# Four graph layers on one core: transposed edges and repeated 1/sums moved from TensorE to DMA, and a fixed row of turns

## The chip, the cores and the metric

The kernel runs on one core of one Trainium2 chip. The metric is the time of one execution on the device in microseconds. Before the change it was 2764.22 us, the median of three runs (2763.69 to 2765.53).

## What is computed

There are 64 graphs with 256 nodes each and 256 features per node, with a symmetric 0/1 matrix of edges `adj` for every graph. Four layers follow each other, and behind each stands x = layernorm(x + layer(x)). All data are f32.

```
# layer 0: attention with 4 heads of 64; masked by adj; output projection; layer norm with gamma, beta
attn = softmax(where(adj == 0, NEG, q @ k.T * 64**-0.5));  out = (attn @ v) @ Wo.T + bo
# layer 1: layer norm; attention with 8 heads of 32, q = k = v = normed x; then an MLP
x = x + attention(layer_norm(x));  x = x + gelu(layer_norm(x) @ W1 + b1) @ W2 + b2        # 256 -> 1024 -> 256
# layer 2: one head; scores leaky_relu(s1[n] + s2[m]), masked, softmax, times Wh = x @ W
# layer 3: one head; scores leaky_relu((x * a0) @ x.T), masked, softmax, times x
```

The reference's layer 3 has four kinds of edges, of which this input has one.

## The kernel before

The kernel takes the graphs in 32 groups of G = 2. `P` is 128, `N` and `D` are 256, `QB` = 2 blocks of 128 nodes per graph, `TB` = 4 blocks per group, `T` = 512 nodes per group and `NC` = 2 chunks of 128 features. Scores are kept with the keys on the partitions, so that the product with v needs no transposition: a softmax is exp, times the mask, and division by the sum afterwards. A group is a Python generator that writes out instructions up to its next `yield`; several groups are run in turns, so that their instructions stand interleaved in the engines' queues. TensorE's order is tied to the order of the program.

The mask is the matrix of edges with the keys first. `adjb` is `adj` in bf16. TensorE transposes it, and VectorE takes the smaller of it and its transpose; the sum tells whether it is symmetric:

```python
pt = ps_m.tile([P, G, QB, N], BF16, name="pm")          # PSUM
for t in range(TB):
    i, q = divmod(t, QB)
    for kc in range(QB):
        transpose(pt[:, i, kc, q * P:(q + 1) * P], adjb[:, t, kc * P:(kc + 1) * P], identb)
mask = act.tile([P, G, QB * N], BF16, name="mask")
nc.vector.scalar_tensor_tensor(mask, pt, 1.0, adjb, ALU.mult, ALU.min, accum_out=both_ways[:, g:g + 1])
yield from rest("mask")
```

In layer 0 each chunk of features holds m = 2 heads. The products with v go into `po[:, 0]`, and the sums of the exponentials into `po[:, 1]`, by a weight `pick` that has a one in column c:

```python
for n, c in enumerate(cs):                              # both chunks of one graph
    po = ps_m.tile([P, 2, N], F32, name="pm")
    ...  # 8 matmuls of 32 rows each: po[r:r + 32, 0, :] from v and e
    for kc in range(QB):
        for h in range(m):
            z = (2 * h + kc) * 32
            matmul(po[z:z + 32, 1, :], pick[:, c, :], es[n][:, h, kc * N:(kc + 1) * N], start=True, stop=True)
    nc.scalar.copy(oT[:, c, :], po[:, 0, :])
    if c == 0:
        nc.scalar.copy(sums, po[:, 1, :])               # zs
    else:
        nc.vector.tensor_tensor(sums, sums, po[:, 1, :], ALU.add)
```

Then the sums are brought to the nodes' partitions, added up, inverted, repeated 64 times for each head, and transposed back, so that `oT` (features first) can be multiplied by them. It is followed by the projection with `woT`:

```python
def behind(i, oT, zs):                                  # layer 0, one graph
    pz = sums_of(zs)                                    # 2 transposes of 128x128
    r = r_0[:, g * G + i]
    nc.vector.tensor_reduce(r..., pz..., AX.X, ALU.add)
    nc.vector.reciprocal(r, r)                          # 128x8
    rr = att.tile([P, QB, D], F32, name="rr")
    nc.vector.tensor_copy(rr..., r...to_broadcast([P, QB * 4, 64]))
    yield
    pr = ps_m.tile([P, NC, N], F32, name="pm")
    for c in range(NC):
        for q in range(QB):
            transpose(pr[:, c, q * P:(q + 1) * P], rr[:, q, c * P:(c + 1) * P], ident)
    nc.vector.tensor_tensor(oT, oT, pr, ALU.mult)
    yield
    ...  # matmuls of oT with woT, then statistics, scaling, two layer norms (z, xb)
```

The matmul with W2 adds b2 by a matmul with `onesb` and a row `b2m` at the end of every block's sum. The groups are started every 15 turns, and each running group gets one step per turn; `rest` puts empty steps in:

```python
PACE = 15
REST = {"xn": 1, "e3": 2, "products 4": 1, "wh": 2, "mask": 2, "products 2": 1, "xT2": 1}
...
while waiting or running:
    if waiting and step % PACE == 0:
        running.append(waiting.pop(0))
        if waiting:
            next(waiting[0])                            # the loads of the next group
    for r in list(running):
        if next(r, END) == END:
            running.remove(r)
    step += 1
```

Behind the MLP a group goes through layers 2 and 3 as one piece: transposition, a projection (`wx`), scores and mask in `qT`, product with the values, statistics and scaling to `xn`, each for both graphs. At the very end a small test of all sums and edges decides whether a general version of the program has to run as well; with this input it does not.

Of the kernel before, what the change touches and what calls it, by code (L numbers as in the profile page):

```python
# [16 lines left out]
P = 128  # L17
N = 256
# [16 lines left out]
PACE = 15  # L35

REST = {"xn": 1, "e3": 2, "products 4": 1, "wh": 2, "mask": 2, "products 2": 1, "xT2": 1}
# [358 lines left out]
def usual_input(ctx: ExitStack, tc: tile.TileContext, a: dict, out: bass.AP, flag: bass.AP):  # L396
# [5 lines left out]

    nc = tc.nc
# [8 lines left out]
    ps_m = ctx.enter_context(tc.tile_pool(name="ps_m", bufs=4, space=bass.MemoryType.PSUM))  # L412

# [3 lines left out]
    identb = const.tile([P, P], BF16, name="identb")  # L417
    nc.vector.tensor_copy(identb, ident)
    mhalf = const.tile([P, 2 * TB], F32, name="mhalf")
    nc.gpsimd.memset(mhalf, -0.5)  # L420

    pick = const.tile([P, NC, 32], F32, name="pick")
    nc.gpsimd.memset(pick, 0.0)
    for c in range(NC):
        nc.gpsimd.memset(pick[:, c, c:c + 1], 1.0)
# [12 lines left out]
    r_0 = const.tile([P, B, QB, 4], F32, name="r_0")  # L438
# [116 lines left out]
    def to_psum(src, c):  # L555

        pt = ps_m.tile([P, T], F32, name="pm")
        for t in range(TB):
            transpose(pt[:, t * P:(t + 1) * P], src[:, t, c * P:(c + 1) * P], ident)
        return pt  # L560

    def transposed(src, scale=None, bias=None):

        dst = act.tile([P, NC, T], F32, name="xT")
        for c in range(NC):
            pt = to_psum(src, c)
            if scale is None:
                nc.scalar.copy(dst[:, c, :], pt)
            else:
                nc.scalar.activation(dst[:, c, :], pt, AF.Identity, bias=bias[:, c:c + 1], scale=scale[:, c:c + 1])  # L570
        return dst
# [30 lines left out]
    def products(i, cs, v, es, hd, oT, sums, gamma=None):  # L602

        m = P // hd
        for n, c in enumerate(cs):
            po = ps_m.tile([P, 2, N], F32, name="pm")
            for kc in range(QB):  # L610
                for r in range(0, P, 32):
                    h = r // hd
                    e = es[n * (m // 2) + h // 2]
                    matmul(po[r:r + 32, 0, :], v[:, i * QB + kc, c * P + r:c * P + r + 32],
                           e[:, h % 2, kc * N:(kc + 1) * N], start=kc == 0, stop=kc == QB - 1)
            if gamma is not None:
                nc.scalar.activation(oT[:, c, :], po[:, 0, :], AF.Identity, scale=gamma[:, c:c + 1])
                continue
            for kc in range(QB):
                for h in range(m):  # L620
                    z = (2 * h + kc) * 32
                    matmul(po[z:z + 32, 1, :], pick[:, c, :], es[n][:, h, kc * N:(kc + 1) * N], start=True, stop=True)
            nc.scalar.copy(oT[:, c, :], po[:, 0, :])
            if c == 0:
                nc.scalar.copy(sums, po[:, 1, :])
            else:
                nc.vector.tensor_tensor(sums, sums, po[:, 1, :], ALU.add)

    def sums_of(zs):

        pt = ps_m.tile([P, QB, P], F32, name="pm")
        for q in range(QB):
            transpose(pt[:, q, :], zs[:, q * P:(q + 1) * P], ident)
        return pt

    def rest(where):

        for _ in range(REST.get(where, 0)):
            yield

    def attention(qT, kT, v, mask, hd, gamma, behind):
# [13 lines left out]
        for i in range(G):  # L655
            for cs in ((0, 1),) if m == 2 else ((0,), (1,)):
# [11 lines left out]
                before = (i, cs, v, es, hd, oT, zs, gamma)  # L668
                yield
                for _ in rest(f"scores {m}"):  # L670
                    go_on()
                    yield
# [3 lines left out]
        yield from rest(f"products {m}")  # L676
# [4 lines left out]
    def project(dst, srcT, w, extra, row=None):  # L681
# [3 lines left out]
        for i in range(G):  # L685
            pm = ps_m.tile([P, QB, D], F32, name="pm")
            for q in range(QB):
                t = i * QB + q
                for c in range(chunks):
                    matmul(pm[:, q, :], srcT[:, c, t * P:(t + 1) * P], w[:, c, :],  # L690
                           start=c == 0, stop=c == chunks - 1 and row is None)
                if row is not None:
                    matmul(pm[:, q, :], onesb, row, start=False, stop=True)
                if chunks > NC:
                    yield
            o = dst[:, i * QB:(i + 1) * QB, :]
            if extra is None:
                nc.scalar.copy(o, pm)
            else:
                nc.vector.tensor_tensor(o, pm, extra[:, i * QB:(i + 1) * QB, 0:D], ALU.add)  # L700

    def layer0(g, x, mask):
# [19 lines left out]

        def behind(i, oT, zs):
            pz = sums_of(zs)
            r = r_0[:, g * G + i]
            nc.vector.tensor_reduce(r.rearrange("p q (c h) -> p q c h", c=NC),
                                    pz.rearrange("p q (h k z) -> p q z h k", h=2, k=QB)[:, :, 0:NC], AX.X, ALU.add)
            nc.vector.reciprocal(r, r)

            rr = att.tile([P, QB, D], F32, name="rr")  # L730
            nc.vector.tensor_copy(rr.rearrange("p q (h d) -> p (q h) d", d=64),
                                  r.rearrange("p q h -> p (q h)").unsqueeze(2).to_broadcast([P, QB * 4, 64]))
            yield
            pr = ps_m.tile([P, NC, N], F32, name="pm")
            for c in range(NC):
                for q in range(QB):
                    transpose(pr[:, c, q * P:(q + 1) * P], rr[:, q, c * P:(c + 1) * P], ident)
            nc.vector.tensor_tensor(oT, oT, pr, ALU.mult)
# [20 lines left out]
        yield from attention(qT, kT, v, mask, 64, None, behind)  # L759
        return xb, z  # L760

    def layer1(xb, z, mask):
# [34 lines left out]
        yield from project(x2, hT, w2, both, b2m)  # L797
        return (yield from renormed(x2))

    def renormed(y, var=None):  # L800
# [3 lines left out]
        for i in range(G):  # L804
# [5 lines left out]
        yield from rest("xn")  # L810
        return xn

    def values_of(e, v, one, x, rs, var=None):

        y = act.tile([P, TB, D], F32, name="y")
        for t in range(TB):
# [9 lines left out]
        return (yield from renormed(y, var))  # L826

    def layer2(x, mask):
        xT = transposed(x)
        yield  # L830
        yield from rest("xT2")
# [3 lines left out]
        for tb in range(TB):  # L835
# [5 lines left out]
        yield from rest("wh")  # L841
# [3 lines left out]
        nc.scalar.activation(ex, wh[:, :, D:D + 3], AF.Exp)  # L845
        pt = ps_m.tile([P, G, N], F32, name="pm")
        for t in range(TB):
            transpose(pt[:, t // QB, t % QB * P:(t % QB + 1) * P], ex[:, t, 0:1].to_broadcast([P, P]), ident)
        e = act.tile([P, G, QB, N], F32, name="qT")
        for t in range(TB):  # L850
            i, kc = divmod(t, QB)
            nc.vector.tensor_scalar(e[:, i, kc, :], pt[:, i, :], ex[:, t, 1:2], ex[:, t, 2:3], ALU.mult, ALU.max)
        nc.vector.tensor_tensor(e.rearrange("p g k q -> p (g k q)"), e.rearrange("p g k q -> p (g k q)"),  # L853
                                mask.rearrange("p g k -> p (g k)"), ALU.mult)
        yield
        return (yield from values_of(e, wh, D + 3, x, small.tile([P, TB], F32, name="r")))

    def layer3(g, x, mask):
        xT = act.tile([P, NC, T], F32, name="xT")
        xa = act.tile([P, NC, T], F32, name="z")  # L860
        for c in range(NC):
            pt = to_psum(x, c)
            nc.scalar.copy(xT[:, c, :], pt)
            nc.scalar.activation(xa[:, c, :], pt, AF.Identity, scale=a0[:, c:c + 1])
        yield
        ps = ps_s.tile([P, G, QB, N], F32, name="ps")
        for i in range(G):
            for kc in range(QB):
                for c in range(NC):
# [5 lines left out]
        nc.scalar.activation(e, ps, AF.Exp, bias=shift)  # L875
        nc.scalar.activation(low, ps, AF.Exp, bias=shift, scale=SLOPE)  # L876
        nc.vector.tensor_tensor(e, e, low, ALU.max)  # L877
        nc.vector.tensor_tensor(e.rearrange("p g k q -> p (g k q)"), e.rearrange("p g k q -> p (g k q)"),
                                mask.rearrange("p g k -> p (g k)"), ALU.mult)
        yield  # L880
        yield from rest("e3")
        return (yield from values_of(e, x, D, x, r_3[:, g], last[:, g]))

    def group(g):
# [8 lines left out]
        pt = ps_m.tile([P, G, QB, N], BF16, name="pm")  # L893
        for t in range(TB):
            i, q = divmod(t, QB)
            for kc in range(QB):
                transpose(pt[:, i, kc, q * P:(q + 1) * P], adjb[:, t, kc * P:(kc + 1) * P], identb)
# [4 lines left out]
        yield from rest("mask")  # L902
        xb, z = yield from layer0(g, x, mask)
        x = yield from layer1(xb, z, mask)
        x = yield from layer2(x, mask)
        x = yield from layer3(g, x, mask)
        nc.sync.dma_start(out[g * G:(g + 1) * G].rearrange("b (q p) d -> p (b q) d", p=P), x[:, :, 0:D])
# [59 lines left out]
    waiting = [group(g) for g in range(B // G)]  # L967
    next(waiting[0])
    preparing = prepare()
    running = []  # L970
    step = 0
    while waiting or running:
        if waiting and step % PACE == 0:
            running.append(waiting.pop(0))
            if waiting:
                next(waiting[0])
        for r in list(running):
            if next(r, END) == END:
                running.remove(r)
        step += 1  # L980
        if step >= PREPARE:
            next(preparing, END)
# [4 lines left out]
    nc.vector.tensor_reduce(tops[:, 0:1], r_0.rearrange("p b q h -> p (b q h)"), AX.X, ALU.add)  # L987
# [49 lines left out]
```

## Time and profile before

| engine | busy us | share of the span |
|---|---|---|
| TensorE matmul (PE) | 2678.1 | 97% |
| TensorE weight load (PEld) | 1842.3 | 67% |
| VectorE (DVE) | 1932.5 | 70% |
| ScalarE (ACT) | 1294.7 | 47% |
| GpSimd (POOL) | 576.8 | 21% |

The profile is of one execution with a span of 2764.3 us. A row of the timeline or of the groups names the line of the kernel, the engine and the operation, then the output and the input with their shapes. All matmuls come from one helper (L521) and all transposes from another (L524), so they are told apart by the names of the tiles: `pm<-ident,rr` is a transposition of `rr`. A matmul of f32 stands as two records. The DMA engines moved 57.78 MB, 21 GB/s over the span, and nearly all of that load in the steady state is x, adj and out.

### The profile page before, as it was taken

Reading aid. Unit: us, or ns where it says so; the run is one execution under the profiler, and the core shown is the slowest. Engines: PE = TensorE matmul, PEld = TensorE weight load, DVE = VectorE, ACT = ScalarE, POOL = GpSimd, SP = SyncE. Lnnn points to the kernel's source line nnn. Section 1 sums busy time; section 2 is a strip of 40 time slices with the busy share of each in tenths; the row PEclk is TensorE's granted clock in tenths of the full one; section 3 lists DMA queues with packets and bytes.
Section 4 is the critical chain, followed back from the end, with each engine's and each line's share of the span. In section 5 each row is a group of like instructions: output and inputs, shape, how many; then the busy total and the mean of one; then the engine's idle time right before and its main releaser. Section 6 shows DMA issues by size and latency. Waiting matters only on the chain.

```text
span 2764.3 us, 45617 instructions
## 1 busy us (share of the span) xinstructions
PE 2678.1 (97%) x17288; PEld 1842.3 (67%) x17288; DVE 1932.5 (70%) x6346; ACT 1294.7 (47%) x1953; POOL 576.8 (21%) x1138
## 2 busy tenths in 40 slices
PE   6999999999999999999999999999999999999986
PEld 3666666666666767666667666666666666666664
DVE  5667776777676777766777767677767776767754
ACT  3444544544544444544445445445444445444441
POOL 1112121221221221212221222222212212222211
PEclk8999999999999999999999999999999999999998
DMA  4000000000000000000000000000000000000000
GB/s 126 16 8 24 16 24 16 24 16 16 24 21 19 16 24 16 24 16 24 16 24 16 24 16 24 16 20 20 24 16 17 23 16 24 9 16 9 9 8 16
DMA packets 57904, 57.78 MB, mean 21 GB/s; under 512 B 5072, under 2 KB 57296, under 8 KB 57680
## 3 DMA queue, kind: packets, MB, share of 16 engines
q1 hardware_dynamic: 56592, 54.28, 6.4%
q8 instruction: 139, 2.28, 0.3%
q14 instruction: 85, 0.70, 0.1%
q10 hardware_dynamic: 1088, 0.53, 0.1%
HBM read 38.02 MB, written 16.78 MB: 20 GB/s over the span
## 4 chain that ended last, share of the span: by engine, by line
PE 68%; DVE 20%; POOL 8%; issue 2%; ACT 1%; DMA 1%; POOLq 0%; SPq 0%; ACTq 0%; DVEq 0%
PE pm L521 53%; PE ps L521 9%; PE pm L524 6%; POOL rstd L544 6%; DVE xn L552 4%; DVE e L597 3%; DVE st L537 3%; POOL ve L540 2%; DVE z L552 1%; DVE e L591 1%; DVE mv L538 1%; ACT e L589 1%; DVE y L750 1%; DVE xb L756 1%; DVE xb L552 1%
## 5 line engine op out<-in xcount | busy, mean ns | idle before, releaser
L589 ACT ACTIVATE e<-ps 128x1024 f32<-128x1024 f32 x384 | 372.2, 1021 | 356.5 <-PE ps L521 353.3
L521 PE MATMUL pm<-L_gnn_W,hT 128*128 128x256 f32 x2048 | 463.2, 379 | 0.0
L521 PE MATMUL pm<-xT,L_gnn_W 128*128 128x512 f32 x1024 | 450.6, 593 | 0.0
L521 PEld LDWEIGHTS pm<-L_gnn_W,hT 128*128 128x128 f32 x2048 | 383.9, 190 | 63.2 <-issue 15.1
L597 DVE SCALAR_TENSOR_TENSOR e<-e,mask 128x256 f32<-128x256 f32 x1024 | 399.3, 454 | 29.1 <-ACT e L589 29.1
L794 ACT ACTIVATE hT<-pm,b 128x512 f32<-128x512 f32 x256 | 175.9, 687 | 477.5 <-PE pm L521 477.5
L540 POOL TENSOR_SCALAR ve<-mv 128x2 f32<-128x2 f32 x384 | 93.1, 243 | 1315.5 <-DVE mv L538 1121.7
L521 PEld LDWEIGHTS pm<-xT,L_gnn_W 128*128 128x128 f32 x1024 | 192.5, 190 | 216.5 <-issue 214.2
L537 DVE BATCH_NORM_STATS2 st<-y 128x6 f32<-128x256 f32 x768 | 300.4, 410 | 5.6
L544 POOL TENSOR_TENSOR rstd<-ve,mhalf 128x2 f32<-128x2 f32 (+1 forms) x384 | 297.9, 776 | 26.6
L552 DVE TENSOR_SCALAR xn<-y,mv,rstd 128x256 f32<-128x256 f32 x384 | 163.5, 472 | 127.2 <-POOL rstd L544 127.2
L877 DVE TENSOR_TENSOR qT<-qT,kT 128x1024 f32<-128x1024 f32 x32 | 39.2, 1226 | 195.1 <-ACT kT L876 195.1
L521 PE MATMUL pm<-e,z 128*32 128x256 f32 x2048 | 149.2, 385 | 3.7 <-DVE e L597 2.9
L521 PE MATMUL pm<-e,v 128*32 128x256 f32 x2048 | 135.5, 382 | 16.9 <-DVE e L591 16.9
L591 DVE TENSOR_TENSOR e<-e,mask 128x1024 f32<-128x1024 f32 x128 | 148.3, 1220 | 0.5 <-ACT e L589 0.5
L521 PE MATMUL ps<-xT 32*128 32x256 f32 x2048 | 147.8, 402 | 0.0
L780 POOL TENSOR_TENSOR both<-y,xb 128x512 f32<-128x512 f32 x64 | 81.7, 1277 | 314.6 <-DVE y L779 314.6
L718 POOL TENSOR_TENSOR x<-x,beta 128x1024 f32<-128x1024 f32 x32 | 75.5, 2359 | 334.9 <-PE pm L524 334.9
L570 ACT ACTIVATE xT<-pm,beta,gamma 128x512 f32<-128x512 f32 x128 | 92.9, 773 | 103.9 <-PE pm L524 103.6
L521 PE MATMUL ps<-qT,kT 64*128 64x256 f32 x1024 | 128.0, 389 | 0.3 <-ACT e L589 0.3
L538 DVE BATCH_NORM_AGGREGATE mv<-st 128x2 f32<-128x6 f32 x768 | 121.6, 171 | 3.0
L521 PE MATMUL pm<-v,qT 128*128 128x260 f32 x512 | 120.3, 389 | 3.3 <-DVE qT L853 3.3
(144 smaller groups left out, 4321.1 us busy)
## 6 DMA issues: line engine op xcount, KB each, us to landing
x<-in_x SPq DMA_DIRECT2D x32, 512.0 KB, 3.8
adj<-in_adj SPq DMA_DIRECT2D x32, 512.0 KB, 3.8
out<-xn SPq DMA_DIRECT2D x32, 512.0 KB, 2.9
L_gnn_W<-in_L_gnn_W SPq DMA_DIRECT2D x2, 1024.0 KB, 8.6
L_gnn_WqT<-in_L_gnn_WqT ACTq DMA_DIRECT2D x1, 256.0 KB, 4.9
L_gnn_WkT<-in_L_gnn_WkT ACTq DMA_DIRECT2D x1, 256.0 KB, 6.8
L_gnn_WvT<-in_L_gnn_WvT SPq DMA_DIRECT2D x1, 256.0 KB, 7.5
L_gnn_WoT<-in_L_gnn_WoT SPq DMA_DIRECT2D x1, 256.0 KB, 7.8
```

What stands on the lines that cost most here:

```text
L521: in_order(nc.tensor.matmul(*args, **kw))
L524: in_order(nc.tensor.transpose(*args))
L537: nc.vector.bn_stats(st[:, q, :], src[:, t, 0:D])
L538: nc.vector.bn_aggr(mv[:, q, :], st[:, q, :])
L540: nc.gpsimd.tensor_scalar(ve[:, 0], mv[:, :, 1], EPS, None, ALU.add)
L544: nc.gpsimd.tensor_tensor(rstd, ve, mhalf[:, 0:k * QB].rearrange("p (k t) -> p k t", k=k), ALU.pow)
L552: nc.vector.tensor_scalar(dst[:, t, 0:D], src[:, t, 0:D], mv[:, q, 0:1], rstd[:, q:q + 1], ALU.subtract, ALU.mult)
L570: nc.scalar.activation(dst[:, c, :], pt, AF.Identity, bias=bias[:, c:c + 1], scale=scale[:, c:c + 1])
L589: nc.scalar.activation(e, ps, AF.Exp, scale=scale)
L591: nc.vector.tensor_tensor(e, e, mask.unsqueeze(1).to_broadcast([P, 2, QB * N]), ALU.mult)
L597: nc.vector.scalar_tensor_tensor(e[:, h, k], e[:, h, k], 1.0, mask[:, k], ALU.mult, ALU.mult, accum_out=sums[:, kc, c, j:j + 1])
L794: nc.scalar.activation(hT[:, f, :], pm, AF.Gelu, bias=b1[:, f:f + 1])
```

## The change

It has five parts. The edges are transposed by DMA from `adjb` to a tile `adjT` in SBUF, so that TensorE and PSUM have no part in the mask. The sums of layer 0 are taken by a weight of 32 columns of ones, one group of 32 rows for each head, with both halves of the keys added up in PSUM; they lie features first from the start, and are inverted there as 128x256. The 1/sums go by DMA as four rows to DRAM, and from there repeated to 64 partitions per head, so no transposition is needed and no copy. The row b2m comes first and for both blocks of a graph in one matmul of 512 columns. The turns are no longer a rhythm with rests: `ORDER` is a fixed row of 44 turns, each naming the age of the group that takes its next step, and it is gone through once for each new group. The last group's graphs go separately through all that follows the MLP's first matmul, the second behind the first by two turns.

```diff
-PACE = 15
-REST = {"xn": 1, "e3": 2, "products 4": 1, "wh": 2, "mask": 2, "products 2": 1, "xT2": 1}
+ORDER = "14202302132441323211321321210212012010021010"
...
+    dram = ctx.enter_context(tc.tile_pool(name="dram", bufs=2, space=bass.MemoryType.DRAM))
-    r_0 = const.tile([P, B, QB, 4], F32, name="r_0")
+    r_0 = const.tile([P, B], F32, name="r_0")
...
# products
+        po = ps_m.tile([P, len(cs), N], F32, name="pm")
         for n, c in enumerate(cs):
-            po = ps_m.tile([P, 2, N], F32, name="pm")
...
-            for kc in range(QB):
-                for h in range(m):
-                    z = (2 * h + kc) * 32
-                    matmul(po[z:z + 32, 1, :], pick[:, c, :], es[n][:, h, kc * N:(kc + 1) * N], start=True, stop=True)
-            nc.scalar.copy(oT[:, c, :], po[:, 0, :])
-            if c == 0:
-                nc.scalar.copy(sums, po[:, 1, :])
-            else:
-                nc.vector.tensor_tensor(sums, sums, po[:, 1, :], ALU.add)
+        pz = ps_m.tile([P, N], F32, name="pm")
+        for kc in range(QB):
+            for h in range(4):
+                matmul(pz[32 * h:32 * h + 32, :], ones[:, 0:32], es[h // 2][:, h % 2, kc * N:(kc + 1) * N],
+                       start=kc == 0, stop=kc == QB - 1)
+        nc.scalar.copy(oT, po)
+        nc.vector.reciprocal(sums, pz)
+        nc.scalar.activation(pz, sums, AF.Copy, accum_out=tally[i])
...
# project
+            if row is not None:
+                matmul(pm, onesb, row.unsqueeze(1).to_broadcast([P, QB, D]), start=True, stop=False)
             for q in range(QB):
...
-                if row is not None:
-                    matmul(pm[:, q, :], onesb, row, start=False, stop=True)
...
# layer 0
-        def behind(i, oT, zs):
-            ...                                         # as above, up to the multiplication
+        def behind(i, oT, rz):
+            rr = att.tile([P, NC, N], F32, name="rr")
+            lines = dram.tile([NC, 2, N], F32, name="lines")
+            nc.sync.dma_start(lines.rearrange("c h n -> (c h) n"), rz[0:P:32, :])
+            for h in range(2):
+                nc.sync.dma_start(rr[h * 64:h * 64 + 64, :, :], lines[:, h, :].unsqueeze(0).to_broadcast([64, NC, N]))
+            yield
+            nc.vector.tensor_tensor(oT, oT, rr, ALU.mult)
             yield
...
# group
-        pt = ps_m.tile([P, G, QB, N], BF16, name="pm")
+        pt = io.tile([P, G, QB, N], BF16, name="adjT", bufs=1)
         for t in range(TB):
             i, q = divmod(t, QB)
-            for kc in range(QB):
-                transpose(pt[:, i, kc, q * P:(q + 1) * P], adjb[:, t, kc * P:(kc + 1) * P], identb)
+            nc.sync.dma_start_transpose(pt[:, i, :, q * P:(q + 1) * P], adjb[:, t, :])
+        yield
...
-        yield from rest("mask")
         xb, z = yield from layer0(g, x, mask)
-        x = yield from layer1(xb, z, mask)
-        x = yield from layer2(x, mask)
-        x = yield from layer3(g, x, mask)
-        nc.sync.dma_start(out[...], x[:, :, 0:D])
+        y, hT, both = yield from layer1(xb, z, mask)
+        def others(gs):                                 # W2, layers 2 and 3 and the output of the graphs gs
+            ...
+        if g < B // G - 1:
+            yield from others(ALL)
+            return
+        parts = [others((i,)) for i in ALL]
+        turn = 0
+        while parts:
+            for r in parts[:turn // QB + 1]:
+                if next(r, END) == END:
+                    parts.remove(r)
+            turn += 1
+            yield
...
# the turns
-    while waiting or running:
-        ...
+    for period in range(len(groups) + int(max(ORDER))):
+        if period + 1 < len(groups):
+            next(groups[period + 1])
+        for age in ORDER:
+            g = period - int(age)
+            if 0 <= g < len(groups):
+                next(groups[g], END)
```

## The prediction

> **What bounds the kernel now.** I read the page's first part, then the stretches of the span, then TensorE's order of work in one period of the steady state, then the waits.
>
> ```profile
> PE 2678.1 (97%) x17288; PEld 1842.3 (67%) x17288; DVE 1932.5 (70%) x6346; ACT 1294.7 (47%) x1953; POOL 576.8 (21%) x1138
> ```
>
> TensorE is busy for 2678.1 of 2764.3 us: only 86.2 us of idle time are left, and no other engine is above 70%. So a gain has to come from TensorE's own work, or from those 86 us. The stretches say where they are (columns: stretch, its length, busy us and instructions of each engine, clock, DMA share, GB/s):
>
> ```profile
> 0.00:69.00 69.00, 41.87 (x284) 26.67 (x285) 37.83 (x110) 26.12 (x40) 12.42 (x30) 0.88 0.45 126
> 600.00:1200.00 600.00, 594.08 (x3828) 407.81 (x3827) 430.25 (x1417) 286.59 (x433) 129.85 (x256) 1.00 0.07 20
> 2600.00:2700.00 100.00, 93.00 (x470) 63.55 (x469) 61.65 (x216) 40.36 (x58) 18.80 (x40) 0.98 0.02 6
> 2700.00:2764.00 64.00, 39.16 (x150) 30.08 (x148) 29.84 (x89) 8.50 (x15) 8.16 (x23) 0.81 0.05 18
> ```
>
> The first 69 us hold 27 us of idle time, the last 164 us hold 32, and the steady state loses about 1% (6 us in 600), some 27 us in all. Next is the timeline of TensorE between two starts of a group (start, us, operation), cut to the rows that the change touches:
>
> ```profile
> 1381.55 1.09 PE L524 MATMUL pm<-ident,x 128*128 128x128 f32 x8
> ...
> 1417.48 1.07 PE L521 MATMUL pm<-e,v 128*32 128x256 f32 x16 [0.55 <-DVE e L591]
> 1418.36 0.62 PE L521 MATMUL pm<-e,pick 128*32 128x256 f32 x8
> 1418.80 1.05 PE L521 MATMUL pm<-e,v 128*32 128x256 f32 x16
> ...
> 1427.12 0.60 PE L524 MATMUL pm<-ident,zs 128*128 128x128 f32 x4
> 1427.56 1.04 PE L524 MATMUL pm<-ident,xb 128*128 128x128 f32 x8
> 1428.65 1.06 PE L524 MATMUL pm<-ident,rr 128*128 128x128 f32 x8
> 1429.56 0.60 PE L524 MATMUL pm<-ident,ex 128*128 128x128 f32 x4
> ...
> 1450.69 0.61 PE L524 MATMUL pm<-identb,adjb 128*128 128x128 bf16 x8
> 1451.13 1.04 PE L524 MATMUL pm<-ident,xn 128*128 128x128 f32 x8
> ...
> 1465.32 1.09 PE L524 MATMUL pm<-ident,x 128*128 128x128 f32 x8
> ```
>
> A period is 1465.32 - 1381.55 = 83.77 us and holds one group. Durations overlap by their modelled ends, so I take the cost of a run of matmuls from its start to the next start.
>
> **What the Trainium skill says.** "TensorE: Matmul & The Clock Gate", section "Packing small matmuls", says that matmuls on different 32-wide tiles of the array run at once. The trace agrees: 16 records of e,z with 32 output rows take 1.00 us, 16 records with 128 rows 3.45. So the four heads' columns of ones run side by side, as pick's already do. "VectorE: DVE Perf Modes", section "Walkthrough: the 8-slice pipeline in each mode", has the reciprocal as an iterated divide with a repeat count of 8. The trace's small ones agree that it is dear: 128x16 takes 248 ns and 128x8 198, thus 6.2 ns an element where a plain 128x256 operation takes 1.6. "Advanced Engine Details and Errata", section "X-Bar Transpose (TRN2)", has transposing DMAs "as fast as regular DMAs"; no run here shows one. "DMA: Bandwidth & Descriptors", section "Two DMAs through the same engine are not ordered", says that a DMA which reads what another wrote must wait for its completion; the built kernel has that wait, so the two hops of the 1/sums add up.
>
> **The change part by part, steady state.** TensorE loses, per group: 8 transposes of edges, 1451.13 - 1450.69 = 0.44 us; 4 of zs, 1427.56 - 1427.12 = 0.44; 8 of rr, 1429.56 - 1428.65 = 0.91. The b2m matmul goes from four of 256 columns to two of 512. From its start to the next start the four take 0.21, 0.20, 0.20 and 0.11 us, 0.72 in all; with half the switches and the same columns I estimate 0.57, so 0.15 less. The sums stay at 8 matmuls per graph: today e,v and pick alternate, and 16 e,v and the pick behind them take 1418.80 - 1417.48 = 1.32, of which pick is 0.44 as against 0.54 the second time; two rounds of 4 heads cost about the same 0.95. Sum: 0.44 + 0.44 + 0.91 + 0.15 = 1.94 us a group, over 32 groups 62 us.
>
> VectorE loses per graph zs+ (0.42), the reduction (0.18), the small reciprocal (0.20) and the copy rr (0.42), 1.22 us; it gains a reciprocal of 128x256, estimated from the slope as 256 x 6.2 ns + 0.15 = 1.75 us. That is 64 x 0.53 = 34 us more on an engine with 830 us to spare. ScalarE changes two copies of 372 ns and one of 379 for one of about 585 and one with a sum of about 0.6: even. Both lie beside TensorE.
>
> **Does the DMA path hide?** By the built order TensorE does, between the second graph's sums and the first matmul with woT: xn,qT 3.6, wx,xT 3.7, xb 1.0, ex 0.45, a quarter of W1 3.4, so 12.2 us. In it go: reciprocal 1.75 (behind the first graph's and 2 us of other VectorE work, say 4), three issues of about 0.45, lines to DRAM about 2.6 (as b2m's small copy lands), rr about 3.8 (as 512 KB of x), multiplication 0.65: 12.4. The first graph is some 3 us ahead. So it is hidden, just, and the second one can hold TensorE or VectorE for a microsecond at worst. The edges' transposes stand half a period before the mask that reads them and cost nothing.
>
> **Waits in the steady state.** Today they are 0.55 (e,v for the mask product) and 0.17 (z) in this period. The new row puts e,z between the scores and e,v, and more work ahead of z, so both should shrink. Against that, ps_m's four buffers now hold pz until ScalarE's sum behind the reciprocal: the fourth xn,qT takes the buffer of the second pz, and adding up VectorE's queue it comes free about 0.8 us late. I take the waits as even to slightly better, -0.1 a period, -3 us in all.
>
> **The start** gets worse. The edges' transposes are issued behind w1 and w2 (issued at 17 us, 8.6 us to landing), so the first mask is there at about 31 to 32 us, where its first product ran at 28.28. VectorE's built order puts the second group's mask ahead of the fourth product, and the lines of the first group stand in the SP queue behind the transposes of groups 1 and 2. Then come two reciprocals and the two hops, with no other TensorE work to fill: the woT matmul, at 40.02 today, should start near 50. Estimate +10 us.
>
> **The end** gets better. From the last transposes of xn at 2713.21 to the end the last group takes 51 us, with only 25 of work, one graph pair in lockstep. Separately, each instruction covers half the rows and the second graph's matmuls fill the first one's waits. The last graph's own chain (statistics 3 us, rstd 1.1 and scaling 0.7 three times, four matmul groups of 1.8, exp, max and mask at half width) adds up to roughly 28 to 30 us behind hT. And xn,qT moves into the gap of 6 us at 2655 to 2671. Estimate -12 us.
>
> Sum: 2764 - 62 - 3 + 10 - 12 = 2697. The row of turns is written out turn by turn, which speaks for one fitted to shorter waits than the 27 us of today; I allow 7 us for that and predict 2690.
>
> **Rivals.** (a) The DMA hops don't hide: multiplication by rr waits in VectorE's queue, and all behind it. For it: 12.4 against 12.2 us. Two us a period would give 60 us back, about 2755. Against it: work for other groups stands between. (b) ScalarE's sum over the reciprocal blocks the ScalarE queue until VectorE is there, and the PSUM buffers go round late: 1 us a period, 2720 to 2725. For it: four buffers, all in use there. Against it: the next ScalarE work is a copy of wx 3.6 us later. (c) The row removes nearly all steady waits and the start loses less: 2764 - 62 - 20 - 12 = 2670.
>
> **Range and chances.** (c) with a shorter end gives 2662; (b) with a dearer start gives 2722. The limit of 2% is 2709, 19 us above my figure and about one standard deviation of what I have left open: faster 0.78, same 0.19, slower 0.03.
>
> **What would show it.** Right: no rows with adjb, zs and rr transposes on TensorE, its busy time 60 to 65 us less at 2613 to 2620; the reciprocal near 1.75 us a time; a period of 81 to 82 us; the first woT matmul at 48 to 53 us; less than 45 us from the last hT to the end. Wrong: waits on rr of more than 1 us each in VectorE's list, or TensorE idle for over 2 us a period.

## The result and the profile after

The changed kernel takes 2714.07 us, the median of four runs (2713.66 to 2715.4), against 2764.7 beside it: a ratio of 0.9818, with a 95% interval of 0.9801 to 0.9835. The predicted time was 2690. The gain is 1.8%; the prediction gave a gain of more than 2% (under 2709 us) a chance of 0.78, and that did not come true. The first part of the page of the kernel after (busy us, share of the span, instructions):

```profile
PE 2643.0 (97%) x16584; PEld 1782.5 (66%) x16584; DVE 1985.5 (73%) x6156; ACT 1292.0 (48%) x1962; POOL 586.7 (22%) x1139
```

TensorE is busy for 35 us less, not for the 60 to 65 that the prediction named. The stretches of the kernel after, with the columns as before:

```profile
0.00:69.00 69.00, 35.42 (x190) 20.96 (x190) 30.52 (x68) 21.45 (x35) 8.42 (x23) 0.79 0.55 151
600.00:1200.00 600.00, 599.28 (x3735) 406.31 (x3734) 451.87 (x1402) 292.47 (x443) 134.90 (x261) 1.00 0.10 30
2550.00:2650.00 100.00, 96.61 (x524) 65.20 (x517) 71.11 (x241) 42.25 (x66) 23.03 (x52) 1.00 0.05 17
2650.00:2711.90 61.90, 41.54 (x172) 32.83 (x170) 31.02 (x92) 10.63 (x24) 8.89 (x26) 0.86 0.06 19
```

The steady state looks full: 0.7 us of idle time in 600, where there were 6. The first 69 us are emptier than before, 34 us of idle time instead of 27. The timeline of TensorE in one period (start, us, operation) says more:

```profile
1368.20 1.09 PE L519 MATMUL pm<-ident,x 128*128 128x128 f32 x8
1369.13 0.38 PE L516 MATMUL pm<-b2m,onesb 128*128 128x512 bf16 x1
1369.34 3.62 PE L516 MATMUL pm<-L_gnn_W,hT 128*128 128x256 f32 x16
1372.89 1.15 PE L516 MATMUL ps<-xT 32*128 32x256 f32 x16
1373.97 2.39 PE L516 MATMUL pm<-e,z 128*32 128x256 f32 x16
1376.28 3.72 PE L516 MATMUL pm<-L_gnn_W,hT 128*128 128x256 f32 x16
...
1384.44 1.07 PE L516 MATMUL pm<-e,z 128*32 128x256 f32 x16
1385.44 3.70 PE L516 MATMUL pm<-xT,L_gnn_WkT 128*128 128x512 f32 x8
...
1414.21 1.03 PE L519 MATMUL pm<-ident,xb 128*128 128x128 f32 x8
1415.08 0.65 PE L519 MATMUL pm<-ident,ex 128*128 128x128 f32 x4
1415.75 3.70 PE L516 MATMUL pm<-xT,L_gnn_W 128*128 128x512 f32 x8
...
1450.04 0.66 PE L519 MATMUL pm<-ident,x 128*128 128x128 f32 x4
```

The period is 1450.04 - 1368.20 = 81.84 us, 1.93 less than before. The rows of adjb, zs and rr are gone. But the first e,z takes 1376.28 - 1373.97 = 2.31 us to the next start, where the second one, with the same matmuls, takes 1.00. So 1.31 us of each period are a wait that counts as busy time, because the row is one group of 16 matmuls. The timeline of all engines at this point shows whom it waits for:

```profile
1370.00 2.36 POOL L705 TENSOR_TENSOR x<-x,beta 128x1024 f32<-128x1024 f32 x1
1370.06 2.77 DVE L547 TENSOR_SCALAR xn<-y,mv,rstd 128x256 f32<-128x256 f32 x2 [1.14 <-POOL rstd L539]
...
1372.75 0.41 DVE L601 SCALAR_TENSOR_TENSOR e<-e,mask 128x256 f32<-128x256 f32 x1
...
1374.61 0.14 PEld L516 LDWEIGHTS pm<-e,z 128*32 128x32 f32 x2 [0.50 <-DVE e L601]
...
1375.30 0.16 PEld L516 LDWEIGHTS pm<-e,z 128*32 128x32 f32 x8 [0.55 <-DVE e L601]
```

The weight loads of e,z wait for layer 1's mask products (L601). Those stand in VectorE's queue behind two scalings to xn, which take 2.77 us; over the run the median of one is 411 ns and the longest 2449. Beside them GpSimd adds beta0 to x (L705) for 2.36 us. As soon as that addition ends (1372.36), the first xn ends too (1372.51).

From the first hT matmul of the first group (118.81 us before, 134.55 after) and of the last (2692.03 and 2650.74) to the end, the difference of the two profiled spans, 52.4 us, divides as follows:

| part | predicted | measured |
|---|---|---|
| start, up to the first hT | +10 | +15.7 |
| 31 groups (the -62 was for 32) | -62 - 3 - 7 | -57.0 (1.84 each) |
| end, from the last group's first hT | -12 | -11.1 |

### The profile page after: what moved, and what is told of

It is laid out like the page before. It is cut to its first block, busy times and chain, and to the rows that moved or that the text cites. A ratio compares the mean times of both kernels' runs of the same rounds, so it can differ in the third digit from the quotient of the medians.

```text
span 2711.9 us, 44575 instructions
## 1 busy us (share of the span) xinstructions
PE 2643.0 (97%) x16584; PEld 1782.5 (66%) x16584; DVE 1985.5 (73%) x6156; ACT 1292.0 (48%) x1962; POOL 586.7 (22%) x1139
## 4 chain that ended last, share of the span: by engine, by line
PE 84%; DVE 11%; POOL 2%; issue 1%; DMA 1%; SPq 1%; ACT 0%; POOLq 0%; DVEq 0%; ACTq 0%
PE pm L516 67%; PE ps L516 11%; PE pm L519 6%; DVE xn L547 3%; DVE e L601 3%; POOL rstd L539 2%; DVE st L532 1%; DVE y L687 1%; SPq L873 1%; POOL ve L535 1%; DVE mv L533 0%; DMA adj<-in_adj 0%; DVE zs L629 0%; DVE y L802 0%; DVE y L730 0%
## 5 line engine op out<-in xcount | busy, mean ns | idle before, releaser
L601 DVE SCALAR_TENSOR_TENSOR e<-e,mask 128x256 f32<-128x256 f32 x1024 | 363.4, 419 | 156.3 <-ACT e L593 156.3
L516 PE MATMUL pm<-xT,L_gnn_W 128*128 128x512 f32 x1024 | 459.3, 596 | 0.5
L547 DVE TENSOR_SCALAR xn<-y,mv,rstd 128x256 f32<-128x256 f32 x384 | 207.0, 567 | 177.6 <-POOL rstd L539 177.6
L516 PE MATMUL pm<-e,z 128*32 128x256 f32 x2048 | 178.5, 386 | 3.8 <-DVE e L601 0.7
L516 PEld LDWEIGHTS ps<-xT 32*128 32x128 f32 x2048 | 93.5, 185 | 73.3 <-issue 67.9
L699 ACT ACTIVATE qT<-pm,bq 128x512 f32<-128x512 f32 x64 | 44.0, 687 | 184.8 <-PE pm L516 184.8
L516 PE MATMUL pm<-e,v 128*32 128x256 f32 x2048 | 125.9, 386 | 5.3 <-DVE e L595 5.3
L516 PE MATMUL pm<-L_gnn_WoT,oT 128*128 128x256 f32 x512 | 118.5, 386 | 10.3 <-DVE oT L718 10.3
L516 PE MATMUL pm<-xn,qT 128*128 128x257 f32 x512 | 122.0, 392 | 6.3 <-DVE qT L857 6.3
```

The lines of the kernel that those rows point to most:

```text
L516: in_order(nc.tensor.matmul(*args, **kw))
L547: nc.vector.tensor_scalar(dst[:, t, 0:D], src[:, t, 0:D], mv[:, q, 0:1], rstd[:, q:q + 1], ALU.subtract, ALU.mult)
L601: nc.vector.scalar_tensor_tensor(e[:, h, k], e[:, h, k], 1.0, mask[:, k], ALU.mult, ALU.mult, accum_out=sums[:, kc, c, j:j + 1])
```

## The experiments

The theory (A): GpSimd's addition holds up VectorE's scaling, and this costs 1.31 us a period. Rivals: (B) the single buffer of adjb, for whose mask ScalarE waits 63.5 us in all, makes the exponentials late; (C) VectorE is simply fuller by its reciprocals of 128x256. For the start there were the transposing DMAs and the two hops of the 1/sums.

**The addition left out.** `beta0` is zero in this input; the kernel doesn't add it.

```diff
-        nc.gpsimd.tensor_tensor(x, x, over_blocks(beta0), ALU.add)
```

> The changed kernel, but x + beta0 on GpSimd is left out (the output lacks beta0, which is 0 in this input); the order on every other engine is the same. Theory A (GpSimd's 2.36 us addition holds up VectorE's scaling of xn, which stands ahead of the mask products, so e,z on TensorE comes 1.3 us late in every period): the long xn (2.45 us) falls back to 0.41, the 16 e,z records that take 2.39 us take 1.0 to 1.1, the period goes from 81.84 to about 80.5 us, the whole to 2670 to 2680. Theory B (ScalarE's exponentials come late because adjb waits for the mask): no change, 2710 to 2716. Theory C (VectorE is simply fuller by the 128x256 reciprocals): no change either.

Measured: 2674.07 us, 0.9667 (0.9651 to 0.9683) of the kernel before. Its timeline at the same point:

```profile
1350.64 0.73 DVE L547 TENSOR_SCALAR xn<-y,mv,rstd 128x256 f32<-128x256 f32 x2 [1.14 <-POOL rstd L539]
1351.30 0.42 DVE L601 SCALAR_TENSOR_TENSOR e<-e,mask 128x256 f32<-128x256 f32 x1
...
1354.55 1.07 PE L516 MATMUL pm<-e,z 128*32 128x256 f32 x16
1355.55 3.72 PE L516 MATMUL pm<-L_gnn_W,hT 128*128 128x256 f32 x16
```

The two xn take 0.73 us, e,z 1.00, and the period is 80.53. The 40 us are about 30 times 1.31, and an xn of over 2 us stands 30 times in the trace of the changed kernel and not once in this one. The wait of ScalarE for the mask is still there (64.5 us), and so are the reciprocals: A holds, B and C fall as causes of this stall.

**Two buffers for adjb.**

```diff
-        adjb = io.tile([P, TB, N], BF16, name="adjb", bufs=1)
+        adjb = io.tile([P, TB, N], BF16, name="adjb", bufs=2)
```

> The changed kernel with two buffers for adjb, so that ScalarE's next adjb doesn't wait for VectorE's mask (63.5 us of wait in all). Theory A: the exponentials are ready 2 us earlier, but VectorE doesn't take them earlier: 2705 to 2716, the start perhaps a few us shorter. Theory B: e,z is on time, period 80.5 us, 2670 to 2680.

Measured: 2715.73 us, 0.9821 (0.9805 to 0.9838). As a test of B this failed: at the start an adjb moved forward (the second one from 29.89 to 22.22 us), but ScalarE still waits 61.1 us for the mask. It is the run before that decides B.

**The edges of the first three groups by TensorE.** The same four DMAs become eight transposes into PSUM, for the start alone.

```diff
+        on_tensor = g < 3
+        pt = ps_m.tile([P, G, QB, N], BF16, name="pm") if on_tensor else io.tile(..., name="adjT", bufs=1)
...
+            if on_tensor:
+                for kc in range(QB):
+                    transpose(pt[:, i, kc, q * P:(q + 1) * P], adjb[:, t, kc * P:(kc + 1) * P], identb)
+            else:
                 nc.sync.dma_start_transpose(pt[:, i, :, q * P:(q + 1) * P], adjb[:, t, :])
```

> The changed kernel, but the edges of groups 0, 1 and 2 are transposed by TensorE as before, all others by DMA. If the start is late because of the transposing DMAs (first mask at 28.6 instead of 12 us, the second one ahead of the fourth mask product at 38.0, the third ahead of the 1/sums' DMA): the first woT matmul moves from 54.4 to about 44 to 47 us, the whole to 2703 to 2707. If the two hops of the 1/sums' DMA make up the delay alone: 52 to 54 us and 2711 to 2714.

Measured: 2704.37 us, 0.9775 (0.9759 to 0.9791). What it takes away is seen in the timeline of the kernel after at its start (SPq is the queue that issues DMAs):

```profile
28.63 1.23 DVE L876 SCALAR_TENSOR_TENSOR mask<-adjT,adjb 128x1024 bf16<-128x1024 bf16 x1 [6.68 <-DMA adjT<-adjb]
...
31.07 5.68 SPq L873 DMA_TRANSPOSE adjT<-adjb  x4
...
38.03 1.22 DVE L876 SCALAR_TENSOR_TENSOR mask<-adjT,adjb 128x1024 bf16<-128x1024 bf16 x1 [4.03 <-DMA adjT<-adjb]
39.18 1.22 DVE L595 TENSOR_TENSOR e<-e,mask 128x1024 f32<-128x1024 f32 x1
...
40.47 5.06 SPq L873 DMA_TRANSPOSE adjT<-adjb  x4
46.21 1.24 SPq L714 DMA_DIRECT2D lines<-zs  x2
49.85 2.68 SPq L716 DMA_DIRECT2D rr<-lines  x4
53.60 0.69 DVE L718 TENSOR_TENSOR oT<-oT,rr 128x512 f32<-128x512 f32 x1 [5.29 <-DMA rr<-lines]
```

VectorE waits twice for a transposing DMA. The second time it is the next group's mask, ahead of the first group's fourth mask product (39.18). The issue of four of these DMAs takes 5 to 6 us of the queue, and the lines stand behind the third four. In the run without them the projection of the first group starts at 41.89 us, earlier than the 44 to 47 expected:

```profile
41.89 6.47 PE L518 MATMUL pm<-L_gnn_WoT,oT 128*128 128x256 f32 x16 [5.37 <-DVE oT L720]
```

The first hT comes at 123.84, 10.7 us earlier than after the change. Of the 15.7 us the other 5.0 remain: the projection still starts 1.9 us later than before, and takes 6.47 instead of 3.69. The latter goes with TensorE's granted clock. Here are the stretches of this projection before the change and in this run, with the columns as before (the clock is the third number from the end):

```profile
40.02:43.80 3.78, 3.78 (x21) 3.27 (x22) 2.43 (x7) 0.00 (x0) 0.00 (x0) 1.00 0.00 0
41.89:48.40 6.51, 6.47 (x16) 4.56 (x16) 2.74 (x8) 0.00 (x0) 0.82 (x2) 0.59 0.12 40
```

The clock is 0.59 where it was 1.00, and 3.69 / 0.59 is 6.3 us. In the kernel after, it is 0.58 at this place. Why less was granted, no run shows.

**The last group together.** All groups go through `others(ALL)`.

```diff
-        if g < B // G - 1:
+        if g < B // G:
             yield from others(ALL)
```

> The changed kernel, but the last group's graphs go together as in every other group. What the separation brings is then the difference: I expect 2722 to 2726, 8 to 12 us more, all of it behind the last group's first matmul with W2 (61.2 us to the end with separation, 70 to 73 without). If the end got shorter by the row of turns instead, the time stays within 3 us of 2714.

Measured: 2727.72 us, 0.9862 (0.9846 to 0.9879). From the last group's first hT (2653.26) to the end it is 72.8 us, where the separated graphs take 61.2, and the kernel before took 72.3: the gain of the end is the separation's. The whole is longer by 13.6 us, somewhat more than the 8 to 12 expected; 11.6 of it lie behind that hT.

**Both cures at once**, with the whole computation: the addition of beta0 on VectorE, and the first three groups' edges on TensorE.

```diff
-        nc.gpsimd.tensor_tensor(x, x, over_blocks(beta0), ALU.add)
+        nc.vector.tensor_tensor(x, x, over_blocks(beta0), ALU.add)
         # and on_tensor = g < 3, as above
```

> The whole computation again: x + beta0 on VectorE (1.2 us, which the built order puts between the two halves of the mask products, where VectorE waits for ScalarE for 1.57 us without the addition), and the edges of groups 0 to 2 on TensorE. If the collision with GpSimd and the late start are separate and both real, their gains add up: 40 + 10 us, 2660 to 2668. If VectorE's extra 1.2 us a period is felt on TensorE: 2690 to 2700.

Measured: **2660.25 us** (2660.14 to 2660.64), 0.9616 (0.9600 to 0.9632), the fastest of all. e,z is back at 1.00. VectorE's addition is one instruction of 1.22 us, in a gap between two halves of the mask products.

**The sums the old way** under the new row: pick, zs, the small reciprocal, rr and its transposes as before; the edges stay with the DMA.

```diff
-        pz = ps_m.tile([P, N], F32, name="pm")
-        ...                                             # ones, reciprocal of 128x256, lines and rr by DMA
+                    matmul(po[z:z + 32, 1, :], pick[:, c, :], es[n][:, h, kc * N:(kc + 1) * N], start=True, stop=True)
+        ...                                             # zs, r, rr and the transposes of both, as before the change
```

> The changed kernel, but layer 0's sums by pick, transposed, inverted, repeated and transposed back on TensorE and VectorE as before, with no DMA. If TensorE's busy time is what counts: 0.44 + 0.91 us more a group, 43 us in all, less about 6 at the start, where the two DMA hops fall away: 2748 to 2756. If the DMA way costs hidden waits in the steady state, less: below 2735.

Measured: 2815.1 us, 1.0176 (1.0159 to 1.0193). Neither reading had that. TensorE's list of waits in this kernel (total us, times, longest) begins:

```profile
PE pm L523 <- DVE zs L635: 63.7, 32, 2.0
```

In the new row the transposes of zs follow right upon the sums, and TensorE waits 2 us a group for VectorE's sum. With the 1.35 us of transposes (32 times, 43 us) the loss is 107; it came to 101. So this row needs the DMA way. Whether another row would suit the old sums, no run shows.

**All edges by TensorE** under the new row (`on_tensor = True` in the edit above).

> The changed kernel, but all edges transposed by TensorE. 0.44 us more a group (14 us over 32 groups), and 10 us less at the start, as with the first three groups on TensorE: 2714 to 2720, thus the DMA transposes alone bring next to nothing in the whole change. If they cost anything hidden in the steady state, below 2710.

Measured: 2703.6 us, 0.9772 (0.9756 to 0.9788): the start's gain, and nothing lost in the steady state. The number is that of the second reading, but not for its reason: the period is 81.84 us whether the edges go by TensorE or by DMA. The transposes' 0.46 us stand ahead of the stalled e,z, which shrinks from 2.31 to 1.90. While TensorE waits there, work in front of the wait costs nothing.

**All edges by TensorE, beta0 on VectorE.** If that reading holds, the same 0.44 us must count once the stall is gone.

> As the version with x + beta0 on VectorE, but all edges transposed by TensorE. With the collision in place the 0.44 us of the edges cost nothing, and my reading is that they filled TensorE's wait for the mask products, which stand right behind them. Then without the collision they must count: 0.44 x 29 groups more than 2660, 2671 to 2676. If transposes of edges on TensorE are free for another reason: 2658 to 2663.

Measured: 2672.91 us, 0.9666 (0.9650 to 0.9682): 12.7 us more than with only the first three groups' edges on TensorE. They do count: 29 groups by 0.44.

**The old turns** with everything else new.

```diff
-ORDER = "14202302132441323211321321210212012010021010"
+PACE = 15
+REST = {"xn": 1, "e3": 2, "products 4": 1, "wh": 2, "mask": 2, "products 2": 1, "xT2": 1}
```

> The changed kernel with the turns of before (a group every 15 turns, with rests). The way from the last sums to woT on TensorE is then 1433.43 - 1423.52 us of before less the transposes that fall away, about 8.5 us, where the chain over the DMA needs about 12: VectorE waits on rr in nearly every period, 2 to 4 us, and TensorE behind it. I expect 2740 to 2800. If the row of turns does nothing for the DMA hops, 2705 to 2725.

Measured: 2790.01 us, 1.0086 (1.0069 to 1.0103). The time lies in the range, the reason does not: VectorE waits for rr 5 times and 10.0 us in all, about as in the kernel after (3 times, 9.0). The period is 84.23, and the first e,z in it takes 2.15.

**The old turns and the old sums**, both edits above, with the edges left to the DMA.

> The turns of before and the sums of before; edges by DMA, b2m first, last group apart. With the old turns and the new sums the profile shows no wait on rr, but waits on xb, z and the mask products behind VectorE's two reciprocals of 1.75 us. If those cause the loss, the old sums under the old turns have none of it: 2764 less 0.44 x 32 = 14 for the edges, 9 for b2m and 11 for the end, plus 8 to 10 at the start, 2735 to 2750. If the old turns are slow for another reason of the new kernel: 2790 plus the transposes of zs and rr, 2810 to 2835.

Measured: 2789.52 us, 1.0087 (1.0070 to 1.0104). Neither range has it. The old sums put 1.34 us of transposes back into a period, but it grows by only 0.32, from 84.23 to 84.55. So under the old turns the new sums gave back about 1.0 us a group in waits: in the run before, the transposes of xb took 1.59 us to the next start, here 1.09, and the first e,v with its sums 3.00, here 2.73. Another 10 us went at the start (first hT at 138.78, here at 129.05). VectorE's reciprocals of 1.75 us stand ahead of xb in its queue, which fits, but no run shows them alone. They aren't the whole of the old turns' loss: the period of 84.55 stands against 83.77 before, though TensorE is rid of the edges, and e,z takes 2.16 instead of 1.27. Its timeline of all engines there:

```profile
1403.39 1.21 DVE L909 SCALAR_TENSOR_TENSOR mask<-adjT,adjb 128x1024 bf16<-128x1024 bf16 x1
1403.46 3.35 POOL L727 TENSOR_TENSOR x<-x,beta 128x1024 f32<-128x1024 f32 x1 [10.82 <-PE pm L524]
1404.52 2.57 DVE L606 SCALAR_TENSOR_TENSOR e<-e,mask 128x256 f32<-128x256 f32 x1
```

And the same place in the kernel before:

```profile
1382.66 1.21 DVE L899 SCALAR_TENSOR_TENSOR mask<-pm,adjb 128x1024 bf16<-128x1024 bf16 x1
1382.73 2.36 POOL L718 TENSOR_TENSOR x<-x,beta 128x1024 f32<-128x1024 f32 x1 [10.94 <-PE pm L524]
1383.79 1.58 DVE L597 SCALAR_TENSOR_TENSOR e<-e,mask 128x256 f32<-128x256 f32 x1
```

The addition took 2.36 us beside a mask that read one input from PSUM (`pm`). Beside one that reads both from SBUF (`adjT`, `adjb`) it takes 3.35, 1 us longer, and the mask product behind it 2.57 instead of 1.58 (the median of all mask products is 0.42). The Trainium skill, "SBUF — State Buffer", section "Who interferes with whom", fits: an instruction of VectorE with two inputs in SBUF contends with one of GpSimd that reads SBUF, the later one is blocked for the other's whole length, and tensor_scalar (xn) can contend too. The trace agrees in the ends: the stretched mask products end 0.3 us after the addition, the stretched xn 0.15 us after it, and the stretched addition ends 2.2 us after the mask product. The run of the old turns alone has the same 3.35 and 2.57. By which of these rules xn is held up, no run shows.

**The edges too the old way.** If that is right, an input of the mask in PSUM must free the old turns of their loss.

```diff
-        pt = io.tile([P, G, QB, N], BF16, name="adjT", bufs=1)
+        pt = ps_m.tile([P, G, QB, N], BF16, name="pm")
...                                                     # on top of the old turns and sums: transposes by TensorE
```

> The old turns with the old sums, and now also all edges transposed by TensorE into PSUM again; of the change only the row b2m and the separate last group are left. Theory: with the old turns GpSimd's x + beta0 starts beside VectorE's mask product, which reads both its inputs from SBUF (adjT and adjb) and makes the addition wait: 3.35 us instead of 2.36, and the first of layer 1's mask products, beside it, 2.57 instead of 1.58; from there the 0.9 us by which e,z is longer (2.16 against 1.27). With one of the inputs in PSUM the addition should be back at 2.36 us, the mask product at about 1.6, e,z at about 1.3, and with TensorE's 0.44 us for the edges the period near 84.1: 2752 to 2772 us. Rival: the longer e,z comes from the turns or from the separate yields, not from the edges' place: e,z stays near 2.1, the period rises to 85.0, 2790 to 2805 us.

Measured: 2750.11 us, 0.9946 (0.9929 to 0.9962), 2 us under the theory's range. Its timeline:

```profile
1378.32 1.21 DVE L913 SCALAR_TENSOR_TENSOR mask<-pm,adjb 128x1024 bf16<-128x1024 bf16 x1
1378.39 2.36 POOL L731 TENSOR_TENSOR x<-x,beta 128x1024 f32<-128x1024 f32 x1 [10.82 <-PE pm L528]
1379.46 1.57 DVE L610 SCALAR_TENSOR_TENSOR e<-e,mask 128x256 f32<-128x256 f32 x1
```

The addition is back at 2.36, the product at 1.57, e,z at 1.17, the period at 83.52. Of this period's 1.03 us, e,z gives 0.99 and the transposes of z behind it 0.48 (1.92 to 1.44), less 0.44 for the edges. Over 31 groups the middle of the run is 29.6 us shorter, and the first hT comes 10.8 us earlier. Under the old turns the edges by DMA cost about 1 us a group in the steady state, where they were meant to save 0.44.

**The kernel before without the addition.**

> The kernel before without x + beta0 on GpSimd (the output lacks beta0, which is 0 in this input). GpSimd's addition ran there too, and stretched one mask product of 0.42 us to 1.58 in a period, but with more time ahead of e,z: TensorE lost only 0.27 us. If the collision was there and mostly hidden: 8 to 10 us less, 2754 to 2760. If it was as dear as in the changed kernel: 2725 to 2735.

Measured: 2754.55 us, 0.9962 (0.9948 to 0.9976), 10.8 us less. The collision was there before, at a place where only these 10.8 us of it were felt. A second one was there too, in the kernel before and in this run, beside GpSimd's other addition (`both`):

```profile
1411.36 1.28 POOL L780 TENSOR_TENSOR both<-y,xb 128x512 f32<-128x512 f32 x1 [3.66 <-DVE y L779]
1411.65 2.13 DVE L552 TENSOR_SCALAR xn<-y,mv,rstd 128x256 f32<-128x256 f32 x4
```

The four scalings take 2.13 us, where two alone take 0.74. One of the four takes 1.17 instead of 0.41, and so it is 30 times in the run. The new row moved xn away from `both`, and beside x + beta0.

Between the two kernels the parts can now be put on one after the other (medians; the comparisons with the kernel before stand above):

| kernel | us |
|---|---|
| before | 2764.7 |
| b2m row first, last group separate | 2750.1 |
| and the edges by DMA | 2789.5 |
| and the sums and 1/sums by DMA | 2790.0 |
| and the fixed row of turns (after) | 2714.1 |

The fixed row is worth 76 us, but on top of all the others: with the old sums it gives 2815.1. It earns them by taking away waits: from the run of the old turns to the kernel after, xb goes from 1.59 to 0.87 us, z from 1.90 to 0.87, and e,v loses its wait of 0.56.

## Why the prediction was right, and where not

The time lies in the range, 24 us above the figure. That it lies so near is in part luck: the row took away some 46 us of waits where 10 were counted, and a collision that nothing in the working had put about 40 back. By its steps:

- **TensorE's work, -62: held in its three large terms.** Edges 0.44, zs 0.44 and rr 0.91 came off. TensorE's period without the stall is 80.53 us (the run without the addition); before, 83.77 less about 1.50 of waits is 82.27. The difference, 1.74, is about the sum of these three terms, 1.79. (Smaller waits are left in both: about 0.2 ahead of rr before, about 0.3 ahead of W1 in the run without the addition.) The term of b2m, 0.15, brought nothing: the four matmuls took 0.72, the two take 0.42 (twice 1369.13 to 1369.34), but three of the four groups of hT became about 0.10 longer each.
- **Waits -3 and row of turns -7: this failed.** 31 groups brought 57.0 us, and 1.74 each are 54; waits gave the other 3 instead of 10. The prediction counted 27 us of steady waits from the idle time. They were about 1.50 in the period read, 46 us over 31 groups: 0.55 ahead of e,v and 0.17 ahead of z were shown as waits, but 0.27 in e,z and 0.51 in z lay inside groups that count as busy. The new row removed nearly all of them, as rival (c) had it, and set one of 1.31 in their place. Nothing in the working looked at what each of VectorE's instructions would stand beside, so GpSimd's addition wasn't in any sum. In the built order it could have been seen: the addition follows rstd in GpSimd's queue, and rstd is what xn waits for, so both start together. That one holds up the other could have been read in the trace before, at the 1.58 us of one mask product. Even the very case was there, in the scaling to xn that GpSimd's addition to `both` stretched to 1.17 us.
- **TensorE's busy time 2613 to 2620: wrong for the same reason.** It is 2643.0, with some 40 us of it the stall; without the addition 2602.6.
- **Do the DMA hops hide? Yes**, against rival (a): VectorE waits for rr 3 times in the whole run, all at the start. The reciprocal takes 1748 ns (predicted 1.75 us). From the issue of the lines to that of rr, which has to wait for them, it is 1.7 us (1405.72 to 1407.38), where 2.6 were reckoned. From the second graph's sums (1407.11) to the end of its multiplication by rr (1417.06) it is 9.95 us, where the prediction had 12.4, and woT starts at 1419.29.
- **Rival (b), the sum on ScalarE:** ScalarE's sum does wait 131.5 us in all, about 2 a graph (69.2 put down to zs, 62.3 to r, which VectorE starts as the second zs ends). TensorE hardly feels it: weight loads wait for this sum 29 times, 4.7 us in all.
- **The start, +10: too small.** +15.7. The first mask at 28.63 was earlier than reckoned (31 to 32), the woT matmul at 54.44 later than 48 to 53. The transposing DMAs brought 10.7 us of it: a group waits for the mask of the next one in VectorE's queue, and the lines for the issues of the third group's. The other 5 are the projection: it starts 1.9 us later than before even without these DMAs, and takes 2.8 us longer at the lower clock.
- **The end, -12: near.** -11.1. From the first matmul behind the last hT (2665.31) it is 46.6 us to the end, where less than 45 was named. The run with the last group together shows that the separation gives 11.6 of this part, so the row gave none of it.

## What to carry to other kernels

Where one engine is busy for 97% of the span, look for waits inside its groups: take each group's time from its start to the next start, compare it with an equal group elsewhere, and read the weight loads and the longest against the median duration of the engines that feed it. When a change moves an operand from PSUM to SBUF, or moves instructions of VectorE beside those of GpSimd, the one may hold up the other, as here, and a saving on the main engine can turn into a loss. Judge a fixed order only together with the operations that it was fitted to.

## What was not expected of the hardware

- GpSimd's f32 addition of 128x1024 stretches one VectorE scaling of 128x256 from 0.41 to 2.45 us, and is itself stretched from 2.36 to 3.35 us by a bf16 mask of VectorE with both inputs in SBUF. Beside a mask that reads PSUM it is not. GpSimd's addition of 128x512 stretches such a scaling to 1.17 us.
- Issuing a transposing DMA of 128x256 bf16 takes 1.24 us of its queue (the median), and four took up to 6.9; a plain one took 0.5 to 0.6. Their transfers are hidden in the steady state, their issues are not hidden at the start.
- VectorE does the addition of 128x1024 f32, for which GpSimd needs 2.36 us, in 1.22.
